# Outer sums of the weight: from adding DMAs to VectorE, in a list-scheduled factorization kernel

## Chip, cores and metric

One core of a Trainium2 chip. The metric is the device time of one execution in microseconds (us); the runs of the kernel before have a median of 1429.27 us (1428.62 to 1429.29, three runs).

## The reference

A factorization machine layer: a linear part, plus half the sum over 64 embeddings of the squared projection less the projection of squares. x is r_x, 1024 x 512; the weight is 64 x 512 x 512; all is float32.

```python
out_lin = x @ lin_w.T + lin_b
xv = jnp.einsum('bf,efm->bem', x, weight)
zp = jnp.einsum('bf,efm->bem', jnp.square(x), jnp.square(weight))
interaction = 0.5 * jnp.sum(jnp.square(xv) - zp, axis=1)
return out_lin + interaction
```

The second einsum needs only the sum of the weight's squares over the embeddings, so its product is small. The first is nearly all of the work.

## The kernel before

**Tiling.** The weight is rearranged on the host into 16 groups of 32 output columns, each a 512 x 2048 matrix (embedding within column). A group is cut into four quadrants w11, w12, w21, w22 (q = 0 to 3 of `weight[g, q]`), each 1 MB as 128 partitions x 2 column blocks x 2 x 512. For each group x times the matrix is made by two levels of a seven-product scheme (Strassen's, in Winograd's form). The outer level has seven products, in the order `ORDER` (line 19). The left operands X1 to X7 are sums of blocks of x, made once in the opening. The right operands are w11, w12, w21, w22 and outer sums: T1 of w11 and w12; T2 of T1 and w22; later w12 is overwritten by a sum with w22, and w21 by a sum with T2 (`outer_sum`, line 417). `RHS` (line 446) says which product i reads which.

**One outer product**, `tree` (line 450): GpSimd makes four inner sums t1 to t4 of the operand's blocks (128 x 512 each, two buffers each). Seven inner products follow, each one "pair" of the planner (`PAIR`, 1.72 in its units of us), which is four matmul instructions in the profile. `PLACE` (line 23) sets their order: product p of step s stands at 7s + PLACE[p], so that the inner products of neighbouring steps are interleaved. Their PSUM banks are b1, b3 and two of b2. Evacuations by ScalarE (`copy`) and VectorE bring the results to SBUF halves (128 x 1024): p5, p53, and the accumulators oa0 to oa3 and ob0 to ob3, one for each position pos of the four. `outer_psum` adds a bank to an accumulator; `outer_sbuf` adds a bank and p5 or p53, then (except where `early(pos)` holds) the accumulator, the latter with both inputs in SBUF. For outer products 2, 4, 5 and 3 `finish` squares the result on ScalarE and reduces it on VectorE into acc. `w_squares` squares and reduces the weight's quadrants likewise.

**early.** For pos 3 of products 2, 7, 4 and 3 the accumulator is added when p5 is evacuated (VectorE, one input in PSUM), so that the last addition with both inputs in SBUF falls away.

**Loads and outer sums before.** `load` brings a quadrant whole by SP's queue. T1 and T2 begin as a load of w11 from HBM into their own buffer, and `load_more` (line 409) then adds w12, or w12 and w22, to it by DMAs that accumulate, issued on GpSimd. w12 gets w22 added in the same way, w21 gets T2. With these sums (and not differences) the signs of X3, X5 and X6 are turned: `x_sum` makes "-a - b" on VectorE.

**The order of the work.** All work is entered in a `Plan` with its engines, a duration per engine, what it reads and writes. `Plan.order` (line 62) gives TensorE's order as fixed by the keys, works back the latest time of every other operation from it, and then steps through time: each engine that is free takes the ready operation with the earliest latest time. An operation that both VectorE and GpSimd can do is taken by VectorE only when it is urgent (line 122). The result is a fixed order for each engine. Lines 151 to 158 let an operation with two SBUF inputs (`both=True`) on VectorE and one on GpSimd lengthen each other:

```python
if e == DVE and o.both and free[POOL] > now + 0.1:
    over = free[POOL] - now
    cost += 0.9 * over
    longer(POOL, 0.35 * over)
elif e == POOL and free[DVE] > now + 0.1 and running[DVE].both:
```

`two_input` (line 272) gives the durations of additions: VectorE 0.08 + 1.06 and GpSimd 0.14 + 2.19 for 128 x 1024; with an input in PSUM, VectorE only. Every addition through it appears in the profile at line 280.

Of the kernel before, what the change touches and what calls it, by code (L numbers as in the profile page):

```python
# [12 lines left out]
AF = mybir.ActivationFunctionType  # L13
ALU = mybir.AluOpType
# [1 line left out]

P = 128
G = 2
ORDER = (1, 6, 2, 7, 5, 4, 3)

SLOT = {1: 0, 7: 1, 2: 2, 4: 3, 5: 4, 6: 5, 3: 6}

# [152 lines left out]
def kernel(  # L175
# [24 lines left out]

    nc = tc.nc  # L210
    NG, NQ, _, NCB, KH, N = weight.shape
    B = xT.shape[1]
# [21 lines left out]
    def make(name, shape, pool=sb):  # L234
        buf[name] = pool.tile(shape, F32, tag=name, name=name)
        return name
# [12 lines left out]
    for i in range(1, 8):  # L249
        make(f"X{i}", [P, 7, Q])  # L250
    for q in ("w11", "w12", "w21", "w22a", "w22b", "T1", "T2"):
        make(q, [P, 2, 2, N])
    for pos in range(4):
        make(f"oa{pos}", half)
        make(f"ob{pos}", half)
# [104 lines left out]

    for i, n in ((1, "A11"), (2, "A12"), (4, "A22")):
        act(block4(i), a_ap(n), None, a_parts(n), (f"X{i}",))

    def x_sum(i, o, a, b, kind, reads, size):

        if kind != "-a - b":
            costs, emit = two_input(o, a, b, kind == "a - b", size)
        else:
            costs = {DVE: two_input(o, a, b, True, size)[0][DVE]}

            def emit(_):
                nc.vector.scalar_tensor_tensor(o, a, -1.0, b, ALU.mult, ALU.subtract)

        plan.add(costs, emit, reads, (f"X{i}",), both=True)

    for i, a, b, kind in (
        (5, "A22", "A21", "a - b"),
        (6, "X5", "A11", "-a - b"),
        (7, "A11", "A21", "a - b"),
        (3, "X6", "A12", "-a - b"),  # L380
    ):
        x_sum(i, block4(i), a_ap(a), a_ap(b), kind, a_parts(a, b), 1024)
    for i in ORDER:
        x = buf[f"X{i}"]
        a11, a21, a12, a22 = (x[:, s, :] for s in range(4))
        s1, s2, s4 = (x[:, s, :] for s in range(4, 7))
        for o, a, b, kind in (
            (s1, a21, a22, "a + b"),
            (s2, s1, a11, "a - b"),
            (s4, a12, s2, "a - b"),  # L390
            (a21, a11, a21, "a - b"),
        ):
            x_sum(i, o, a, b, kind, (f"X{i}",), 256)
    for n in a_buf.values():
        plan.add({SP: 0.0}, None, (), (n,) + tuple((n, r) for r in range(KH)))
    for n in ("ob0", "ob1", "ob2", "ob3", "c_0", "c_1"):
# [5 lines left out]
    def w(g, q):  # L402
        return q + "ab"[g % 2] if q == "w22" else q

    def load(g, q):
        n = w(g, QUAD[q])
        dma(buf[n], weight[g, q], (), (n,), 4.8)

    def load_more(n, src, reads=()):

        plan.add(
            {POOL: 1.0},
            lambda _: nc.gpsimd.dma_start(buf[n], src, accum_op=ALU.add),  # L413
            (n,) + reads, (n,), land=8.0,
        )

    def outer_sum(g, which):
        if which < 3:
            n = f"T{which}"
            dma(buf[n], weight[g, 0], (), (n,), 4.8)  # L420
            for q in (1, 3)[:which]:
                load_more(n, weight[g, q])
        elif which == 3:
            load_more("w12", weight[g, 3])
        else:
            load_more("w21", buf["T2"], ("T2",))

    def w_squares(g, q):
        row, col = divmod(QUAD.index(q), 2)
        for c in range(NCB):  # L430
            n, sq = w(g, q), wsq_ring()
            act(buf[sq], buf[n][:, c], AF.Square, (n,), (sq,), 1.07)
            m = g * MG + (2 * col + c) * MI
            reduce(w2_sum[:, ts(row, KH), m:m + MI], buf[sq], (sq,), (("w2", row, m),))

# [6 lines left out]
        reduce(buf[acc_name[g]][:, b:b + G, m:m + MI], buf[n], (n,), ((acc_name[g], i, pos),))  # L442

    ADDEND = {6: "oa", 2: "oa", 7: "ob", 4: "oa", 3: "ob"}
    TARGET = {1: "oa", 6: "ob", 2: "oa", 7: "oa", 4: "oa", 3: "ob"}
    RHS = {1: "w11", 2: "w21", 3: "w22", 4: "w21", 5: "T1", 6: "T2", 7: "w12"}
    acc_name = {}
    acc_parts = [(i, pos) for i in (2, 3, 4, 5) for pos in range(4)]

    def tree(s, g, i):  # L450
        r = w(g, RHS[i])
        b11, b21, b12, b22 = (buf[r][:, c, k, :] for c in range(NCB) for k in range(KH))
        t = {k: t_ring[k]() for k in range(1, 5)}
        for k, a, b, reads in (
            (1, b12, b11, (r,)),
            (2, b22, buf[t[1]], (r, t[1])),
            (3, b22, b12, (r,)),
            (4, b21, buf[t[2]], (r, t[2])),
        ):
            costs, emit = two_input(buf[t[k]], a, b, True, 512)  # L460
            plan.add({POOL: costs[POOL]}, emit, reads, (t[k],))
        rhs = {
            1: (b11, r), 2: (b21, r), 3: (b22, r), 4: (buf[t[4]], t[4]),
            5: (buf[t[1]], t[1]), 6: (buf[t[2]], t[2]), 7: (buf[t[3]], t[3]),
        }

        def product(p, b, first):
            op, name = rhs[p]

            def emit(_):  # L470
                for j in range(G):
                    nc.tensor.matmul(  # L472
                        buf[b][:, j, :], buf[f"X{i}"][:, SLOT[p], ts(j, P)], op,
                        start=first, stop=True, skip_group_check=True,
                    )

            plan.add({PE: PAIR}, emit, (name, f"X{i}", b), (b,), key=7 * s + PLACE[p])

        def copy(o, b):
            act(buf[o], buf[b], None, (b,), (o,))  # L480

        def target(pos):
            return f"{TARGET[i]}{pos}"

        def early(pos):

            return pos == 3 and i in (2, 7, 4, 3)

        def outer_psum(b, pos):

            if i == 1:
                copy(f"oa{pos}", b)
            elif i == 5:
                o = c_ring()
                whole(o, f"oa{pos}", b, psum=True)
                whole(f"ob{pos}", f"ob{pos}", b, psum=True)
                finish(g, i, o, pos)
            else:
                o = target(pos)
                whole(o, b, f"{ADDEND[i]}{pos}", psum=True)  # L500
                if i in (2, 4, 3):
                    finish(g, i, o, pos)

        def outer_sbuf(b, p, pos):

            if i == 1:
                whole(f"oa{pos}", b, p, psum=True)
            elif i == 5:
                o = c_ring()
                whole(p, b, p, psum=True)  # L510
                whole(o, f"oa{pos}", p)
                whole(f"ob{pos}", f"ob{pos}", p)
                finish(g, i, o, pos)
            else:
                a, o = f"{ADDEND[i]}{pos}", target(pos)
                if early(pos):
                    whole(o, b, p, psum=True)
                else:
                    z = p if o == a else o
                    whole(z, b, p, psum=True)  # L520
                    whole(o, z, a)
                if i in (2, 4, 3):
                    finish(g, i, o, pos)

        b2, p5, p53 = b2_ring(), p5_ring(), p53_ring()
        product(5, "b3", True)
        if early(3):
            whole(p5, "b3", f"{ADDEND[i]}3", psum=True)
        else:
            copy(p5, "b3")  # L530
        product(3, "b3", False)
        copy(p53, "b3")
        product(1, "b1", True)
        copy(b2, "b1")
        product(6, b2, False)
        outer_sbuf(b2, p53, 1)
        product(2, "b1", False)
        outer_psum("b1", 0)
        product(7, b2, False)
        outer_sbuf(b2, p5, 3)  # L540
        product(4, b2, False)
        outer_psum(b2, 2)

    for g in range(NG):
        acc_name[g] = acc_ring()
        load(g, 0)
        outer_sum(g, 2)
        for q in (1, 2, 3):
            load(g, q)
        outer_sum(g, 1)  # L550
        w_squares(g, "w12")
        for idx, i in enumerate(ORDER):
            if i == 1:
                w_squares(g, "w11")
            if i == 2:
                w_squares(g, "w21")
            if i == 7:
                outer_sum(g, 3)
            if i == 4:
                outer_sum(g, 4)  # L560
            if i == 5:
                w_squares(g, "w22")
            tree(7 * g + idx, g, i)
        if g + 1 < NG:
            names = tuple((acc_name[g], *k) for k in acc_parts)
            dma(acc_dram[:, :, ts(g, MG)], buf[acc_name[g]], names, names + (("accd", g),))


    for n in ("w11", "w12", "w21", "T1", "T2", w(NG, "w22")):
        for c in range(2):  # L570
            buf[n, c] = buf[n][:, c]
        plan.add({SP: 0.0}, None, (), (n, (n, 0), (n, 1)))
    xe = {(h, q): (("w11", "w12")[h], q) for h in range(2) for q in range(2)}
    last = acc_name[NG - 1]
    edge = M - MG
    acc_all = tuple((n, c) for n in ("T2", w(NG, "w22")) for c in range(2))
    lin_all = tuple((n, c) for n in ("w21", "T1") for c in range(2))
    for (h, q), n in xe.items():
        dma(buf[n], x_src[:, ts(q, KH), ts(h, H)], (), (n,))
    for g in range(NB // G):  # L580
# [85 lines left out]
```

## Time and profile before

| | |
|---|---|
| median of three runs | 1429.27 us |
| profiled execution, its own time | 1429.27 us |
| its span, first to last instruction | 1427.5 us |
| granted TensorE clock, mean | 0.999 |
| TensorE busy | 1409.1 us (99%), 3264 matmuls |
| VectorE (DVE) busy | 1115.5 us (78%), 946 instructions |
| GpSimd (POOL) busy | 1010.6 us (71%), 703 instructions |
| ScalarE (ACT) busy | 678.8 us (48%), 692 instructions |
| DMA: accumulating and other transfers issued by GpSimd | 84.15 MB |
| DMA: transfers issued by SP and ACT | 115.09 MB |
| read from HBM | 177.34 MB |

The span is the time between the first and the last instruction on the chip; the execution's own time lies a little above it. In the profile's rows an engine is followed by the line, the operation, and "out<-in" by the tiles' names without their numbers (p stands for p5 and p53, b for the PSUM banks, t for the inner sums). A row's "idle before" is how long the engine stood before these instructions, and what it waited for.

### The profile page before, as it was taken

Reading aid. Unit: us, or ns where it says so; the run is one execution under the profiler, and the core shown is the slowest. Engines: PE = TensorE matmul, PEld = TensorE weight load, DVE = VectorE, ACT = ScalarE, POOL = GpSimd, SP = SyncE. Lnnn points to the kernel's source line nnn. Section 1 sums busy time; section 2 is a strip of 40 time slices with the busy share of each in tenths; the row PEclk is TensorE's granted clock in tenths of the full one; section 3 lists DMA queues with packets and bytes.
Section 4 is the critical chain, followed back from the end, with each engine's and each line's share of the span. In section 5 each row is a group of like instructions: output and inputs, shape, how many; then the busy total and the mean of one; then the engine's idle time right before and its main releaser. Section 6 shows DMA issues by size and latency. Waiting matters only on the chain.

```text
span 1427.5 us, 10368 instructions
## 1 busy us (share of the span) xinstructions
PE 1409.1 (99%) x3264; PEld 617.9 (43%) x3264; DVE 1115.5 (78%) x946; ACT 678.8 (48%) x692; POOL 1010.6 (71%) x703
## 2 busy tenths in 40 slices
PE   8999999999999999999999999999999999999998
PEld 3434444444444444444444444444444444444443
DVE  1779597886968779696877959788696978969785
ACT  1446354454635446364544635445463544636431
POOL 5886786857768686785958678685777868677660
PEclk9999999999999999999999999999999999999999
DMA  9656381745628175472836638274573817546331
GB/s 306 202 155 173 91 203 45 196 122 143 167 75 205 67 177 151 118 177 63 209 89 164 163 96 199 55 193 113 147 177 91 187 53 185 143 120 145 94 112 60
DMA packets 47286, 200.96 MB, mean 141 GB/s; under 512 B 19008, under 2 KB 20032, under 8 KB 24704
## 3 DMA queue, kind: packets, MB, share of 16 engines
q0 software_dynamic: 11600, 84.15, 30.2%
q1 hardware_dynamic: 35056, 115.09, 23.3%
q10 hardware_dynamic: 576, 1.05, 0.2%
q8 instruction: 27, 0.44, 0.1%
q14 instruction: 27, 0.22, 0.0%
HBM read 177.34 MB, written 6.16 MB: 129 GB/s over the span
## 4 chain that ended last, share of the span: by engine, by line
PE 92%; DMA 2%; POOL 2%; DVE 2%; issue 1%; ACT 0%; DVEq 0%; SPq 0%; ACTq 0%; POOLq 0%
PE b L472 90%; DMA T<-weight 2%; PE b L617 2%; DVE p L280 1%; POOL t L280 1%; POOL X L280 1%; DMA oa<-xT 0%; POOL ob L280 0%; DVE ob L280 0%; ACT X L293 0%; SPq L309 0%; POOL w L413 0%; DVE w22a L280 0%; DVEq L662 0%; ACTq L309 0%
## 5 line engine op out<-in xcount | busy, mean ns | idle before, releaser
L472 PE MATMUL b<-t,X 128*128 128x512 f32 x1792 | 806.1, 592 | 1.7 <-DVE ob L280 1.4
L472 PEld LDWEIGHTS b<-t,X 128*128 128x128 f32 x1792 | 339.2, 190 | 432.1 <-issue 419.9
L472 PE MATMUL b<-w,X 128*128 128x512 f32 x768 | 358.5, 592 | 3.4 <-DVE p L280 2.3
L280 POOL TENSOR_TENSOR t<-w 128x512 f32<-128x512 f32 x128 | 163.2, 1278 | 147.5 <-PE b L472 84.5
L472 PEld LDWEIGHTS b<-w,X 128*128 128x128 f32 x768 | 145.7, 190 | 187.8 <-issue 175.1
L293 ACT COPY p<-b 128x1024 f32<-128x1024 f32 x160 | 160.4, 1002 | 133.6 <-PE b L472 133.6
L295 ACT ACTIVATE oa<-oa 128x1024 f32<-128x1024 f32 x128 | 133.6, 1056 | 166.8 <-DVE oa L280 166.8
L280 POOL TENSOR_TENSOR t<-w,t 128x512 f32<-128x512 f32 x128 | 164.9, 1289 | 57.5 <-PE b L472 57.3
L472 PE MATMUL b<-T,X 128*128 128x512 f32 x384 | 180.4, 592 | 0.0
L302 DVE TENSOR_REDUCE acc<-oa 128x16 f32<-128x1024 f32 x128 | 152.1, 1208 | 18.0 <-ACT oa L295 18.0
L302 DVE TENSOR_REDUCE w_sum<-wsq 128x16 f32<-128x1024 f32 x128 | 152.8, 1204 | 0.2 <-ACT wsq L295 0.2
L293 ACT COPY b<-b 128x1024 f32<-128x1024 f32 x112 | 112.4, 1004 | 82.2 <-PE b L472 82.2
L280 DVE TENSOR_TENSOR oa<-b,p 128x1024 f32<-128x1024 f32 x96 | 116.6, 1214 | 34.7 <-PE b L472 34.7
L295 ACT ACTIVATE wsq<-w 128x1024 f32<-128x1024 f32 x96 | 98.0, 1054 | 70.0 <-DVE w_sum L302 66.5
L280 POOL TENSOR_TENSOR t<-T 128x512 f32<-128x512 f32 x64 | 83.5, 1305 | 47.5 <-issue 33.2
L295 ACT ACTIVATE c<-c 128x1024 f32<-128x1024 f32 x64 | 65.8, 1055 | 106.7 <-DVE c L280 102.8
L472 PEld LDWEIGHTS b<-T,X 128*128 128x128 f32 x384 | 73.0, 190 | 91.8 <-issue 88.2
L280 DVE TENSOR_TENSOR p<-b,p 128x1024 f32<-128x1024 f32 x80 | 97.3, 1216 | 17.9 <-PE b L472 17.9
L280 DVE TENSOR_TENSOR ob<-b,p 128x1024 f32<-128x1024 f32 x48 | 58.5, 1218 | 65.0 <-PE b L472 65.0
L295 ACT ACTIVATE ob<-ob 128x1024 f32<-128x1024 f32 x64 | 67.6, 1058 | 87.3 <-DVE ob L280 87.3
L280 DVE TENSOR_TENSOR oa<-b,oa 128x1024 f32<-128x1024 f32 x64 | 77.8, 1216 | 29.8 <-PE b L472 29.8
L280 POOL TENSOR_TENSOR t<-T,t 128x512 f32<-128x512 f32 x64 | 82.0, 1281 | 25.5 <-PE b L472 25.5
(55 smaller groups left out, 1328.4 us busy)
## 6 DMA issues: line engine op xcount, KB each, us to landing
w<-weight SPq DMA_DIRECT2D x48, 1024.0 KB, 4.9
T<-weight POOLq DMA_DIRECT2D x48, 1024.0 KB, 8.2
T<-weight SPq DMA_DIRECT2D x32, 1024.0 KB, 4.8
w<-weight POOLq DMA_DIRECT2D x16, 1024.0 KB, 10.8
w<-T POOLq DMA_DIRECT2D x16, 1024.0 KB, 6.9
w22a<-weight SPq DMA_DIRECT2D x8, 1024.0 KB, 6.1
w22b<-weight SPq DMA_DIRECT2D x8, 1024.0 KB, 5.9
w<-xT SPq DMA_DIRECT2D x4, 512.0 KB, 4.7
```

The costliest lines, as they stand in the source:

```text
L280: f(o, a, b)
L293: nc.scalar.copy(o, i)
L295: nc.scalar.activation(o, i, func)
L302: lambda _: nc.vector.tensor_reduce(o, i.rearrange("p a (m e) -> p a m e", e=E), axis=AX.X, op=ALU.add),
L472: nc.tensor.matmul(buf[b][:, j, :], buf[f"X{i}"][:, SLOT[p], ts(j, P)], op, start=first, stop=True, skip_group_check=True,)
L617: nc.tensor.matmul(buf[bank][:, j, :], buf[xe[h, k // KH]][:, k % KH, ts((g * G + j) % (NB // 2), P)], w2_sum[:, k, :], start=(k == 0), st ...
```

## The change

The diff, cut to its core. T1, T2 and the two later sums are made by VectorE from the loaded quadrants, as differences; each quadrant and each T becomes two tiles of half the size (suffix .0 and .1), with a load, a square and a sum each; `x_sum` with its turned signs goes, and the block sums of X may all be taken by either engine; `early` goes; product 4 comes before product 5; product 4 now ends in one of the c buffers and product 5 in oa, in place, where it was the other way round. `Plan`, `two_input`, `act` and `reduce` are the same in both.

```diff
-ORDER = (1, 6, 2, 7, 5, 4, 3)
+ORDER = (1, 6, 2, 7, 4, 5, 3)
...
     for q in ("w11", "w12", "w21", "w22a", "w22b", "T1", "T2"):
-        make(q, [P, 2, 2, N])
+        for c in range(NCB):
+            make(f"{q}.{c}", half)
...
-        (5, "A22", "A21", "a - b"),
-        (6, "X5", "A11", "-a - b"),
-        (7, "A11", "A21", "a - b"),
-        (3, "X6", "A12", "-a - b"),
...
+    for i, a, b, sub in ((5, "A21", "A22", 0), (6, "X5", "A11", 1), (7, "A11", "A21", 1), (3, "A12", "X6", 1)):
+        costs, emit = two_input(block4(i), a_ap(a), a_ap(b), sub)
+        plan.add(costs, emit, a_parts(a, b), (f"X{i}",), both=True)
...
-    def load(g, q):
-        n = w(g, QUAD[q])
-        dma(buf[n], weight[g, q], (), (n,), 4.8)
-
-    def load_more(n, src, reads=()):
-
-        plan.add(
-            {POOL: 1.0},
-            lambda _: nc.gpsimd.dma_start(buf[n], src, accum_op=ALU.add),
-            (n,) + reads, (n,), land=8.0,
-        )
+    def load(g):
+        for q in (0, 1, 3, 2):
+            for c in range(NCB):
+                n = f"{w(g, QUAD[q])}.{c}"
+                dma(buf[n], weight[g, q][:, c], (), (n,))
 
     def outer_sum(g, which):
-        if which < 3:
-            n = f"T{which}"
-            dma(buf[n], weight[g, 0], (), (n,), 4.8)
-            for q in (1, 3)[:which]:
-                load_more(n, weight[g, q])
-        elif which == 3:
-            load_more("w12", weight[g, 3])
-        else:
-            load_more("w21", buf["T2"], ("T2",))
+        o, a, b = {
+            1: ("T1", "w12", "w11"),
+            2: ("T2", w(g, "w22"), "T1"),
+            3: ("w12", w(g, "w22"), "w12"),
+            4: ("w21", "w21", "T2"),
+        }[which]
+        for c in range(NCB):
+            whole(f"{o}.{c}", f"{a}.{c}", f"{b}.{c}", True, DVE)
...
-    TARGET = {1: "oa", 6: "ob", 2: "oa", 7: "oa", 4: "oa", 3: "ob"}
+    TARGET = {1: "oa", 6: "ob", 2: "oa", 7: "oa", 3: "ob"}
...
         def target(pos):
-            return f"{TARGET[i]}{pos}"
-
-        def early(pos):
-
-            return pos == 3 and i in (2, 7, 4, 3)
+            return f"{TARGET[i]}{pos}" if i in TARGET else c_ring()
...
             elif i == 5:
-                o = c_ring()
-                whole(o, f"oa{pos}", b, psum=True)
-                whole(f"ob{pos}", f"ob{pos}", b, psum=True)
-                finish(g, i, o, pos)
+                for n in (f"oa{pos}", f"ob{pos}"):
+                    whole(n, n, b, psum=True)
+                finish(g, i, f"oa{pos}", pos)
...
                 a, o = f"{ADDEND[i]}{pos}", target(pos)
-                if early(pos):
-                    whole(o, b, p, psum=True)
-                else:
-                    z = p if o == a else o
-                    whole(z, b, p, psum=True)
-                    whole(o, z, a)
+                z = p if o == a else o
+                whole(z, b, p, psum=True)
+                whole(o, z, a)
...
-        if early(3):
-            whole(p5, "b3", f"{ADDEND[i]}3", psum=True)
-        else:
-            copy(p5, "b3")
+        copy(p5, "b3")
...
-        load(g, 0)
+        load(g)
+        outer_sum(g, 1)
         outer_sum(g, 2)
-        for q in (1, 2, 3):
-            load(g, q)
-        outer_sum(g, 1)
         w_squares(g, "w12")
```

More of the change, by code (lines that the diff above doesn't have):

```diff
@@ L362 @@
         act(block4(i), a_ap(n), None, a_parts(n), (f"X{i}",))
-    def x_sum(i, o, a, b, kind, reads, size):
-        if kind != "-a - b":
-            costs, emit = two_input(o, a, b, kind == "a - b", size)
-        else:
[L369 to L376, printed above, removed]
-        (5, "A22", "A21", "a - b"),
-        (6, "X5", "A11", "-a - b"),
-        (7, "A11", "A21", "a - b"),
-        (3, "X6", "A12", "-a - b"),
-    ):
-        x_sum(i, block4(i), a_ap(a), a_ap(b), kind, a_parts(a, b), 1024)
+    for i, a, b, sub in ((5, "A21", "A22", 0), (6, "X5", "A11", 1), (7, "A11", "A21", 1), (3, "A12", "X6", 1)):
+        costs, emit = two_input(block4(i), a_ap(a), a_ap(b), sub)
+        plan.add(costs, emit, a_parts(a, b), (f"X{i}",), both=True)
     for i in ORDER:
@@ L386 @@
         s1, s2, s4 = (x[:, s, :] for s in range(4, 7))
[L387 to L393, printed above, removed]
+        for o, a, b, sub in ((s1, a21, a22, 0), (s2, s1, a11, 1), (s4, a12, s2, 1), (a21, a11, a21, 1)):
+            costs, emit = two_input(o, a, b, sub, 256)
+            plan.add(costs, emit, (f"X{i}",), (f"X{i}",), both=True)
     for n in a_buf.values():
@@ L430, in w_squares @@
         for c in range(NCB):
-            n, sq = w(g, q), wsq_ring()
-            act(buf[sq], buf[n][:, c], AF.Square, (n,), (sq,), 1.07)
+            n, sq = f"{w(g, q)}.{c}", wsq_ring()
+            act(buf[sq], buf[n], AF.Square, (n,), (sq,), 1.07)
             m = g * MG + (2 * col + c) * MI
@@ L450, in tree @@
     def tree(s, g, i):
-        r = w(g, RHS[i])
-        b11, b21, b12, b22 = (buf[r][:, c, k, :] for c in range(NCB) for k in range(KH))
+        r = [f"{w(g, RHS[i])}.{c}" for c in range(NCB)]
+        b11, b21, b12, b22 = (buf[r[c]][:, k, :] for c in range(NCB) for k in range(KH))
         t = {k: t_ring[k]() for k in range(1, 5)}
         for k, a, b, reads in (
[L455 to L458, printed above, removed]
+            (1, b12, b11, (r[0], r[1])),
+            (2, b22, buf[t[1]], (r[1], t[1])),
+            (3, b22, b12, (r[1],)),
+            (4, b21, buf[t[2]], (r[0], t[2])),
         ):
@@ L462, in tree @@
         rhs = {
-            1: (b11, r), 2: (b21, r), 3: (b22, r), 4: (buf[t[4]], t[4]),
+            1: (b11, r[0]), 2: (b21, r[0]), 3: (b22, r[1]), 4: (buf[t[4]], t[4]),
             5: (buf[t[1]], t[1]), 6: (buf[t[2]], t[2]), 7: (buf[t[3]], t[3]),
@@ L508, in outer_sbuf @@
             elif i == 5:
-                o = c_ring()
                 whole(p, b, p, psum=True)
-                whole(o, f"oa{pos}", p)
-                whole(f"ob{pos}", f"ob{pos}", p)
-                finish(g, i, o, pos)
+                for n in (f"oa{pos}", f"ob{pos}"):
+                    whole(n, n, p)
+                finish(g, i, f"oa{pos}", pos)
             else:
                 a, o = f"{ADDEND[i]}{pos}", target(pos)
-                if early(pos):
-                    whole(o, b, p, psum=True)
-                else:
-                    z = p if o == a else o
-                    whole(z, b, p, psum=True)
-                    whole(o, z, a)
+                z = p if o == a else o
+                whole(z, b, p, psum=True)
+                whole(o, z, a)
                 if i in (2, 4, 3):
@@ L526, in tree @@
         product(5, "b3", True)
-        if early(3):
-            whole(p5, "b3", f"{ADDEND[i]}3", psum=True)
-        else:
-            copy(p5, "b3")
+        copy(p5, "b3")
         product(3, "b3", False)
@@ L566 @@
             dma(acc_dram[:, :, ts(g, MG)], buf[acc_name[g]], names, names + (("accd", g),))
[L569 to L573, printed above, removed]
+    xe = {(h, q): (f"w11.{q}", f"w12.{q}")[h] for h in range(2) for q in range(2)}
     last = acc_name[NG - 1]
     edge = M - MG
-    acc_all = tuple((n, c) for n in ("T2", w(NG, "w22")) for c in range(2))
-    lin_all = tuple((n, c) for n in ("w21", "T1") for c in range(2))
+    acc_all = ("T2.0", "T2.1", w(NG, "w22") + ".0", w(NG, "w22") + ".1")
+    lin_all = ("w21.0", "w21.1", "T1.0", "T1.1")
     for (h, q), n in xe.items():
```

## The prediction

> **What bounds the kernel now.** I read the granted clock first (0.999, so nothing is lost there), then the chain of waits that ended last, then one steady group of weights as a stretch, then VectorE and GpSimd in order of time inside it. The chain in order of time, from the steady part:
>
> ```profile
> 534.41 82.68 PE b L472 x192
> 617.10 0.03 issue
> 617.12 0.02 DVEq L280
> 617.14 0.58 issue
> 617.72 1.22 DVE p L280
> 618.94 0.04 issue
> 618.99 82.68 PE b L472 x192
> ```
>
> The reader should see that TensorE is the path: 192 matmuls in a row, one touch of VectorE, 192 again, repeating every 84.55 us. 82.68/192 is 0.4306 us a matmul; a group has 196, so 84.40 us is TensorE's own, and a group is held up by 0.15 us only. All 3264 matmuls at 0.4306 are 1405.5 us of the span of 1427.5; the other 22.0 are the head (6.0 before the first matmul), the opening and the tail. So the change can gain almost nothing in the steady part and can lose there if VectorE or GpSimd run out of idle time. How much they have, in that stretch:
>
> ```profile
> core 0: us, PE busy (x) PEld busy (x) DVE busy (x) ACT busy (x) POOL busy (x), PEclk, DMA share, GB/s
> 618.99:703.53 84.54, 84.38 (x196) 37.05 (x196) 68.08 (x58) 42.20 (x43) 61.47 (x44) 1.00 0.54 139
> ```
>
> VectorE is idle for 16.5 us of 84.5, GpSimd for 23.1, ScalarE for 42.3. Now the kind of operation the change adds. One VectorE addition with both inputs in SBUF is left in each group, and this is it, VectorE's rows and then GpSimd's:
>
> ```profile
> 696.53 1.21 DVE L302 TENSOR_REDUCE acc<-c 128x16 f32<-128x1024 f32 x1
> 697.65 3.56 DVE L280 TENSOR_TENSOR c<-oa,p 128x1024 f32<-128x1024 f32 x1
> 701.14 1.21 DVE L302 TENSOR_REDUCE w_sum<-wsq 128x16 f32<-128x1024 f32 x1
> 702.27 1.21 DVE L280 TENSOR_TENSOR p<-b,ob 128x1024 f32<-128x1024 f32 x1
> ```
>
> ```profile
> 697.52 2.61 POOL L280 TENSOR_TENSOR ob<-ob,p 128x1024 f32<-128x1024 f32 x1
> 700.08 2.27 POOL L280 TENSOR_TENSOR t<-w22b,t 128x512 f32<-128x512 f32 x1
> ```
>
> The same shape with one input in PSUM takes 1.21 us; this one takes 3.56, because it stands still until GpSimd's 2.61 us operation ends at 700.1, and then GpSimd's next (1.27 us elsewhere) takes 2.27. Each side waits for the other's instruction. The evacuation right behind it, p<-b,ob at 702.27, is the one that TensorE waits for at 703.5: one such addition per group, and one stall per group of 0.15 us.
>
> The Trainium skill says the same of the mechanism (SBUF — State Buffer, Who interferes with whom): a VectorE instruction with two SBUF inputs competes with a GpSimd instruction that reads SBUF, and the loser blocks wholly. By that rule alone the eight new sums would only queue with GpSimd: 61.5 - 4.3 + 9.4 + 8 x 1.2 = 76.2 us of 84.5, and nothing would be lost. The row of 3.56 us speaks against leaving it there, since VectorE stands idle while it queues, and the sum below goes by the rows.
>
> **The change part by part**, per group of 84.54 us.
>
> Rows of the groups that give prices:
>
> ```profile
> L280 DVE TENSOR_TENSOR c<-oa,p 128x1024 f32<-128x1024 f32 x15 | 53.7, 3581 | 0.0
> L280 DVE TENSOR_TENSOR p<-b,oa 128x1024 f32<-128x1024 f32 x32 | 38.9, 1216 | 36.3 <-PE b L472 36.3
> L280 POOL TENSOR_TENSOR oa<-p,oa 128x1024 f32<-128x1024 f32 x32 | 75.5, 2358 | 10.1 <-DVE p L280 8.2
> L280 POOL TENSOR_TENSOR t<-w 128x512 f32<-128x512 f32 x128 | 163.2, 1278 | 147.5 <-PE b L472 84.5
> L413 POOL DMA_DIRECT2D T<-weight x48 | 41.1, 856 | 5.2 <-DMA T<-weight 5.2
> ```
>
> 1. Adding DMAs removed: 48 + 16 + 16 issues on GpSimd over 16 groups, 5 each at 0.86: GpSimd -4.3 us. Two of six whole loads on SP's queue go and the four left become eight halves. The DMA engines are busy 0.54 of the stretch and no steady wait of TensorE names a DMA, so this gains nothing directly.
>
> 2. Eight sums (T1, T2, w12, w21, two halves each) on VectorE alone, both inputs in SBUF. Lower end: 1.21 each, the PSUM row, as if GpSimd were never in the way: 9.7. Upper end: 3.58 each, the row of c<-oa,p: 28.6. In between: GpSimd will have 28 operations of 1.27 and 14 of 2.36 per group, 68.6 us, so 0.81 of the time it is in one; what is left of it is (28 x 1.27² + 14 x 2.36²)/(2 x 68.6) = 0.90 on average, so a wait of 0.73 and 1.94 for a sum: 15.5. I take this, since the planner is free to place the sums and VectorE has gaps, where the one seen sits behind the longest kind.
>
> 3. The early merges undone (pos 3 of products 2, 7, 4, 3): four p<-b,oa or p<-b,ob leave VectorE, -4.9; four copies of 1.00 go to ScalarE, 46.2 of 84.5, hidden; four more additions of 2.36, most on GpSimd, +9.4.
>
> 4. GpSimd held by the eight sums: in the rows above 2.61 for 2.37 (the same addition just before it) and 2.27 for 1.27, so 1.24 each: +9.9 (lower end 0).
>
> Sums: VectorE 68.1 - 4.9 + 15.5 = 78.7 (72.9 to 91.8); GpSimd 61.5 - 4.3 + 9.4 + 9.9 = 76.5. Both at 90% or more, each in a fixed order, with TensorE needing banks back. How tight: by PLACE the bank b2 is read by VectorE between pairs 7s+3 and 7s+6, and 7s+6 and 7s+9, and b1 between 7s+4 and 7s+7, two pairs of 1.72 us free each, so 3.44 - 1.21 - some 0.3 of handing over leaves 1.9 us. A sum of 3.58 ahead of an evacuation overruns that, one of 1.94 ahead of a waiting one just about. Behind the late evacuation, the next product into that bank waits, and with it all of TensorE.
>
> 5. The order 4, 5 for 5, 4. w21 is read by product 2's last pair at 7s+4, then w21 - T2 is made, then GpSimd's first tree operation, then product 4, now two steps on, starts at 7s+8: three pairs, 5.2 us. Unhindered the chain is 0.4 (what GpSimd's rows behind TensorE stand idle) + 1.21 + 0.1 + 1.27 + 0.1 = 3.1; with the two rows of the collision 0.4 + 3.58 + 0.1 + 2.27 + 0.1 = 6.5. So 0 to 1.3 a group; I take 0.2, near the bottom, since the sum is short of time and the planner puts it first.
>
> 6. Stall per group, which no row shows for nine such additions. Lower end 0. Upper end VectorE's 91.8 - 84.4 = 7.4. I take 9 times the 0.17 that TensorE waits today behind one of them, 1.5, plus 0.2 from part 5: 1.7, near the lower row because the stretch still has 5.8 us of VectorE idle by the middle price. That is 1.55 more than now, over 16 groups 24.8 us.
>
> 7. Opening: TensorE now stands 1.10, 2.29 and 0.28 us, the last two after GpSimd waited 4.59 us for an adding DMA. That wait goes: up to -2.6. In its place four sums, and two block sums of X that may go to GpSimd at 2.63 us: up to +5.3, with GpSimd busy 34.0 of the 41 us from 36 to 77. I take 0. Tail: the last 1.41 us wait on VectorE stays, 0 (-1.4 to +2).
>
> Sum: span 1427.5 + 24.8 = 1452.3. The profiled execution took 1429.27 us by its own time, 1.77 above its span, and that is also the median of the runs: 1454.
>
> **The rivals.** (a) All hidden, and a little faster: the sums fall into the half of the group where VectorE now idles (16.5 us), GpSimd is rid of its issues and the opening of its DMA wait. At best the 2.4 us of steady stalls and 2.6 of the opening go: 1424; at worst nothing moves: 1432. For it: both engines stay below the group's length; against it: 3.56 for 1.21, and a stall behind it. It decides if the sums average no more than some 1.5 us and none stands before an evacuation. (b) VectorE becomes the bound: sums near 3.58 each, 91.8 per group: 16 x 7.4 = 118 more, 1547; half of it, 1488 to 1500, if the planner dodges some. For it: fifteen rows of fifteen took 3.56 to 3.60; against it: all fifteen are the same place in the order. (c) The words speak of a scheduler told of the contention, but lines 151 to 158 stand in both versions and the durations in two_input and reduce are not touched: then that part does nothing, and what acts is sums on VectorE, as costed.
>
> **How the numbers follow.** About 0.2% is what this kernel's measurement can tell from no change, 2.9 us. Forecast, a stall of 0.33 to 4.6 us a group: 0.71, 1432 to 1500. Rival (a): 0.17, of which 0.08 below 1426.4 and 0.09 inside 0.2%. Rival (b), above 1500: 0.12; (c) moves no time of its own. Slower is 0.83. The range 1430 to 1500 leaves out most of (a) and (b).
>
> **What would show it.** Right: one-input evacuations still 1.21, eight sums a group at 1.6 to 2.6 us, GpSimd's operations lengthened beside them, VectorE above 76 us a group, and the chain cut into several pieces per group by VectorE or GpSimd instead of one. Wrong: still 192 matmuls unbroken (rival a), or VectorE without idle time and groups of 90 us (rival b). If the loss sits in the first 77 us, part 7 was mis-sized; if TensorE waits for t after w21, part 5.

## The result and the profile after

The changed kernel takes 1438.50 us (median of 4 runs, 1438.25 to 1438.61) against 1429.13 for the kernel before on the same chip (4 runs): a ratio of 1.0066, 95% interval 1.0048 to 1.0083. It is slower, as forecast, but by 9.4 us where the prediction had 24.8. The profiled execution took 1438.61 us, its span 1436.8 against 1427.5 before.

The chain of waits of the changed kernel, in order of time (start, length, what), one group of the steady part. "issue" is time in which an engine waited for nothing that the profile shows, POOLq is the queue of GpSimd; where the chain goes from one engine to another in mid-operation, it shows only the end of that operation:

```profile
634.18 79.25 PE b L438 x184
713.43 0.03 POOLq L274
713.46 0.60 POOL t L274
714.06 3.30 POOL oa L274
717.36 0.02 issue
717.38 0.02 ACT oa L289
717.40 0.94 issue
718.34 1.00 ACT p L287
719.34 0.04 issue
719.39 79.25 PE b L438 x184
```

There is still one break per group, and a group is 85.21 us where it was 84.55. But it is another break than before: no longer a VectorE evacuation, but GpSimd's addition to oa, then a square on ScalarE, then ScalarE's copy to p5. TensorE's own wait there is 0.82 us (0.17 before). The same stretch as a whole:

```profile
core 0: us, PE busy (x) PEld busy (x) DVE busy (x) ACT busy (x) POOL busy (x), PEclk, DMA share, GB/s
634.14:719.35 85.21, 84.38 (x196) 37.15 (x196) 76.27 (x62) 46.50 (x47) 69.36 (x42) 1.00 0.17 51
```

TensorE's 84.38 us are unchanged; VectorE has 8.9 us left and GpSimd 15.9. So neither is full. What goes wrong is in the order of time at the end of the group, VectorE first, then GpSimd, ScalarE and TensorE:

```profile
706.08 1.21 DVE L274 TENSOR_TENSOR w12.1_75<-w22a.1_79,w12.1_75 128x1024 f32<-128x1024 f32 x1
...
711.16 1.77 DVE L274 TENSOR_TENSOR T1.0_82<-w12.0_74,w11.0_72 128x1024 f32<-128x1024 f32 x1
712.86 2.28 DVE L274 TENSOR_TENSOR ob<-ob,p 128x1024 f32<-128x1024 f32 x1
715.06 3.36 DVE L274 TENSOR_TENSOR T2.0_84<-w22a.0_78,T1.0_82 128x1024 f32<-128x1024 f32 x1
```

```profile
706.31 3.21 POOL L274 TENSOR_TENSOR oa<-oa,p 128x1024 f32<-128x1024 f32 x1
709.48 2.38 POOL L274 TENSOR_TENSOR ob<-ob,p 128x1024 f32<-128x1024 f32 x1
711.80 2.25 POOL L274 TENSOR_TENSOR t<-w11.1_73 128x512 f32<-128x512 f32 x1
714.02 3.33 POOL L274 TENSOR_TENSOR oa<-oa,p 128x1024 f32<-128x1024 f32 x1
```

```profile
711.74 1.00 ACT L287 COPY b<-b 128x1024 f32<-128x1024 f32 x1 [0.18 <-PE b L438]
717.38 1.06 ACT L289 ACTIVATE oa<-oa 128x1024 f32<-128x1024 f32 x1 [4.64 <-POOL oa L274]
718.34 0.99 ACT L287 COPY p<-b 128x1024 f32<-128x1024 f32 x1
```

```profile
719.39 1.98 PE L438 MATMUL b<-w11.1_73,X 128*128 128x512 f32 x4 [0.82 <-ACT p L287]
```

Read it from the bottom. TensorE needs bank b3 back from the copy to p5 for the next group's first product. The copy stands behind the square of oa on ScalarE, which has waited 4.64 us for GpSimd's addition to oa. GpSimd is done with that addition late because three of its last four operations took 3.21, 2.25 and 3.33 us for 2.37, 1.27 and 2.37: at each, a VectorE addition with two SBUF inputs was running or next in turn (w12.1, T1.0, and the addition to ob). In these rows VectorE and GpSimd take strict turns. T1.0, from 711.16, stands until ob<-ob,p ends at 711.86, then runs; GpSimd's t, from 711.80, stands until T1.0 ends at 712.93; VectorE's ob stands until t ends at 714.05; and so on. Each turn costs GpSimd 0.84 to 0.98 us.

The difference of the spans, 9.3 us, from TensorE's rows in both profiles: 15 times (0.82 - 0.17) in the steady part, +9.75; the first matmul at 7.90 us instead of 5.96, +1.94; the opening's stalls of 2.29 and 0.28 gone, -2.57; the linear part 30.23 instead of 30.43, -0.2; two single waits of 0.4 and 0.2 that are new, both near the end, +0.6. Together 9.5.

### The profile page after: what moved, and what is told of

Read it like the earlier page. It is cut to its first block, busy times and chain, and to the rows that moved or that the text cites. A ratio compares the mean times of both kernels' runs of the same rounds, so it can differ in the third digit from the quotient of the medians.

```text
span 1436.8 us, 10763 instructions
## 1 busy us (share of the span) xinstructions
PE 1408.8 (98%) x3264; PEld 619.3 (43%) x3264; DVE 1245.7 (87%) x1006; ACT 748.8 (52%) x756; POOL 1149.6 (80%) x691
## 4 chain that ended last, share of the span: by engine, by line
PE 90%; POOL 4%; DVE 2%; issue 1%; ACT 1%; DMA 1%; DVEq 0%; POOLq 0%; SPq 0%
PE b L438 86%; POOL oa L274 3%; PE b L325 2%; PE b L565 2%; ACT p L287 1%; POOL t L274 1%; DMA ob<-lin_wT 0%; DVE p L274 0%; DMA T1.1_83<-lind 0%; DVE ob L274 0%; DVE w11.1_73 L536 0%; DVE w21.0_76 L274 0%; DVE oa L274 0%; DVE acc L296 0%; DVE w11.0_72 L536 0%
## 5 line engine op out<-in xcount | busy, mean ns | idle before, releaser
L287 ACT COPY p<-b 128x1024 f32<-128x1024 f32 x224 | 225.6, 1007 | 266.1 <-PE b L438 226.8
L438 PE MATMUL b<-w21.0_76,X 128*128 128x512 f32 x256 | 120.3, 592 | 0.0
L274 POOL TENSOR_TENSOR oa<-oa,p 128x1024 f32<-128x1024 f32 x32 | 102.8, 3212 | 1.8
L274 POOL TENSOR_TENSOR oa<-p,oa 128x1024 f32<-128x1024 f32 x32 | 75.7, 2365 | 27.2 <-DVE p L274 26.9
L274 POOL TENSOR_TENSOR c<-c,oa 128x1024 f32<-128x1024 f32 x32 | 75.4, 2357 | 13.8 <-DVE c L274 11.7
L274 POOL TENSOR_TENSOR oa<-oa,ob 128x1024 f32<-128x1024 f32 x32 | 76.4, 2387 | 6.9 <-DVE oa L274 6.9
L274 POOL TENSOR_TENSOR ob<-ob,oa 128x1024 f32<-128x1024 f32 x32 | 76.3, 2384 | 5.5 <-DVE ob L274 5.5
L274 POOL TENSOR_TENSOR ob<-p,ob 128x1024 f32<-128x1024 f32 x32 | 75.7, 2364 | 0.5 <-DVE p L274 0.5
L296 DVE TENSOR_REDUCE acc<-ob 128x16 f32<-128x1024 f32 x64 | 75.9, 1209 | 0.0
L296 DVE TENSOR_REDUCE acc<-c 128x16 f32<-128x1024 f32 x64 | 74.8, 1208 | 1.1 <-ACT c L289 1.1
```

Source lines behind the costliest of these rows:

```text
L274: f(o, a, b)
L287: nc.scalar.copy(o, i)
L296: lambda _: nc.vector.tensor_reduce(o, i.rearrange("p a (m e) -> p a m e", e=E), axis=AX.X, op=ALU.add),
L438: nc.tensor.matmul(buf[b][:, j, :], buf[f"X{i}"][:, SLOT[p], ts(j, P)], op, start=first, stop=True, skip_group_check=True,)
```

## The experiments

Each is the changed kernel with one edit, unless it says otherwise; the time of the kernel before beside them was 1428.9 to 1429.8 us.

**The copy first.** The order is the planned one; only two neighbours on ScalarE change places.

```diff
+        if tag[a] == ("sq", 5) and tag[b] == ("p5", 1):
...
+            seq[a:b + 1] = seq[a + 1:b + 1] + [seq[a]]
```

> Edit: on ScalarE the copy that evacuates b3 to p5 for product 1 goes ahead of the square of product 5's oa that now stands before it; nothing else moves. Theory Q (the loss is a wait in ScalarE's fixed order: the square waits 4.6 us for GpSimd's held addition, the copy behind it is late, TensorE stands 0.82 us a group): the 15 stalls of 0.82 go, 1438.5 - 12.3 = 1426 (1425 to 1428), the chain runs through 196 matmuls a group with 0.2 us or less of stall. Rival C (VectorE and GpSimd are short of room as such, and this copy only happens to be what is late first): the stall comes back a few pairs later, 1434 to 1439.

Measured: 1424.41 us, ratio to the kernel before 0.9964 (0.9951 to 0.9977). The chain runs without a break through nearly all groups:

```profile
46.36 1281.38 PE b L439 x2980
```

So rival C falls: nothing else comes late. In that chain a group of 196 matmuls takes 1281.38/2980 x 196 = 84.28 us; against it the break costs 85.21 - 84.28 = 0.93 a group, 14.0 us over 15 groups, which is what the exchange gained (1438.50 - 1424.41 = 14.1). But theory Q was not wholly right either. ScalarE's rows of this run:

```profile
710.85 1.01 ACT L287 COPY p<-b 128x1024 f32<-128x1024 f32 x1 [4.64 <-POOL oa L274]
711.76 1.06 ACT L289 ACTIVATE oa<-oa 128x1024 f32<-128x1024 f32 x1
```

The copy, put first, waits the same 4.64 us for the same addition. p5 has two buffers, and product 5's, two steps back, is the one the copy writes: GpSimd's addition still reads it. The exchange gained one ScalarE instruction, about a microsecond, and that was enough.

**Which of the two holds the copy.** p5 in three buffers (the third holds the bias in the opening), the planner still planning with two: once in the order of the changed kernel, once with the copy first.

```diff
+    p5_real = ring("p5r", 3, half)
...
+        buf[p5] = buf[p5_real()]
```

> Edit: the changed kernel in its own order, but with p5 in three buffers in turn instead of two (the third holds the bias in the opening); the planner still plans with two. In e1_copy_first the copy that was put first still waited 4.6 us for GpSimd's oa addition, which reads the p5 buffer that the copy is to write. Theory F (both waits hold: the square waits for the addition's output, the copy for its input buffer; the square in front costs one ScalarE instruction on top): with the buffer free the square still stands in front, 1437 to 1439, 0.8 us a group. Rival G (the buffer alone is the wait): 1421 to 1426.

> Edit: three p5 buffers and the copy put ahead of the square. Theory F: only with both is the copy free: it starts some 4 us earlier against TensorE's need than in e1_copy_first, without a wait for GpSimd; the time is TensorE's floor as there, 1421 to 1425. Rival: the copy still waits for GpSimd, by something else.

Measured: 1438.55 (0.8 us a group at the copy, as before the edit) and 1422.22 us. In the second, ScalarE's copy is free of GpSimd:

```profile
705.70 1.01 ACT L294 COPY p5r<-b 128x1024 f32<-128x1024 f32 x1 [0.72 <-PE b L446]
709.63 1.06 ACT L296 ACTIVATE oa<-oa 128x1024 f32<-128x1024 f32 x1 [2.92 <-POOL oa L281]
```

TensorE needs the bank at 710.65 in that run, so the copy has 4 us to spare. Theory F holds: two waits for one GpSimd addition, one for its output (the square) and one for its input (the buffer). Taking away either alone leaves the other.

**Which sums cost.** Half sums on VectorE are replaced by a copy of the same size with one SBUF input (the difference is left out, T or w holds one operand); the order stays. The edit, here with the condition of the first of these runs; the others differ in the condition alone:

```diff
             whole(f"{o}.{c}", f"{a}.{c}", f"{b}.{c}", True, DVE)
+            if which < 3:
+                x, y = buf[f"{o}.{c}"], buf[f"{a}.{c}"]
+                plan.ops[-1].emit = lambda _, x=x, y=y: nc.vector.tensor_reduce(
+                    x.rearrange("p a (m e) -> p a m e", e=1),
+                    y.rearrange("p a (m e) -> p a m e", e=1), axis=AX.X, op=ALU.add
+                )
```

> Edit: the four half sums T1 and T2 of each group become VectorE reductions over one element, a copy of the same size with one input in SBUF, so T1 and T2 hold w12 and w22 alone; the order is that of the changed kernel. Theory Q: these four are the ones that stand beside GpSimd's additions of product 5; they take 1.2 us each, GpSimd's oa addition 2.4 for 3.3, the stall of 0.82 goes: 1426 to 1428. Rival P (each SBUF sum costs its share, as the prediction took it, 9.3 us over eight sums): half the loss, 1433 to 1435.

> Edit: as the run before, but for the other four half sums, w12 - and w21 -, which become copies of one input; T1 and T2 stay sums. Theory Q: they stand elsewhere in the group, nothing is gained, 1438.5 within 1, stall still 0.8 a group at the copy to p5. Rival P: half the loss, 1433 to 1435.

Measured: 1424.30 and 1421.97 us. The second was a miss: w12's half 1 does stand beside those operations of GpSimd, at 706.08 ahead of the first. Either four take away all of the stall (TensorE's rows name no steady wait in either run), 14.2 and 16.5 us, so that the two gains together are about twice what is lost. A share per sum can't do that; a threshold can, and theory S was made from it:

> Edit: six of the eight half sums become copies of one input (both of T2 and of w21, T1's half 1, w12's half 0); only T1's half 0 and w12's half 1 stay sums. Theory S (the loss is a threshold: GpSimd's run of four operations up to product 5's last oa addition is held about a microsecond each by w12's half 1, T1's half 0 and the addition to ob on VectorE, the square and the copy behind it come 0.82 us too late, and sums that stand elsewhere cost nothing): 1437 to 1439, TensorE still stands 0.8 us a group at the copy to p5. Rival P (shares): six eighths of the loss go, 1426 to 1429.

> Edit: one of the eight half sums, w12's half 1, becomes a copy of one input; the other seven stay sums. Theory S: GpSimd's run comes 0.85 us earlier, more than the 0.82 that TensorE waits, so all of the loss goes with this one: 1421 to 1426. Rival P: an eighth goes, 1436 to 1438.

> Edit: one of the eight half sums, T1's half 0, becomes a copy of one input; the other seven stay sums. Theory S: as with w12's half 1, all of the loss goes: 1421 to 1426. Rival P: 1436 to 1438.

Measured: 1437.42 with six of eight replaced, 1423.06 with w12's half 1 alone, 1423.95 with T1's half 0 alone. TensorE's waits with six replaced (engine, line, released by: total, times, longest), the same 16 as in the changed kernel:

```profile
PE b L444 <- ACT p L287: 13.5, 16, 1.1
```

and GpSimd and ScalarE with w12's half 1 alone replaced:

```profile
699.24 2.37 POOL L274 TENSOR_TENSOR oa<-oa,p 128x1024 f32<-128x1024 f32 x1
...
705.11 3.34 POOL L274 TENSOR_TENSOR oa<-oa,p 128x1024 f32<-128x1024 f32 x1
```

```profile
708.48 1.06 ACT L289 ACTIVATE oa<-oa 128x1024 f32<-128x1024 f32 x1 [2.82 <-POOL oa L274]
```

The first addition takes 2.37 again for 3.21. GpSimd's run is 0.84 us shorter from there on, and that covers the 0.82. With T1's half 0 replaced the first addition still takes 3.21, and it is t that is short again:

```profile
705.16 1.26 POOL L274 TENSOR_TENSOR t<-w11.1_73 128x512 f32<-128x512 f32 x1
```

It takes 1.26 us for 2.25 with TensorE's products around it unchanged, so its length was VectorE's doing and not a wait for TensorE, from which the chain above enters it. Six sums cost 1.1 us between them, which the intervals of the two runs do not tell from nothing, and each of two single ones decides over 15: 15.4 and 14.6.

The runs of the changed kernel without a steady stall lie between 1422.0 and 1424.6 us. A group of unbroken matmuls takes 84.14 us in the run with the planner's delay below, 84.18 with w12's half 1 replaced, 84.28 with the exchange, 84.31 with the old order restored. Most of this difference is stalls too short for a row to name. TensorE's starts with the exchange, and then with the planner's delay:

```profile
710.16 1.88 PE L439 MATMUL b<-w22b.0_80,X 128*128 128x512 f32 x4
711.91 1.99 PE L439 MATMUL b<-w11.1_73,X 128*128 128x512 f32 x4
713.74 1.88 PE L439 MATMUL b<-t,X 128*128 128x512 f32 x4
```

```profile
709.66 1.88 PE L436 MATMUL b<-w22b.0_80,X 128*128 128x512 f32 x4
711.38 1.88 PE L436 MATMUL b<-w11.1_73,X 128*128 128x512 f32 x4
713.10 1.88 PE L436 MATMUL b<-t,X 128*128 128x512 f32 x4
```

Undisturbed products start 1.72 us apart. With the exchange the product that reuses the bank starts 1.75 us after the one before it, and the next 1.83 us later: 0.14 us lost, which is 84.28 - 84.14. The copy there ends at 711.86, just before the start at 711.91. So even a copy in time to 0.05 us costs a little, and a break costs more than the wait that its row names: 85.21 - 84.14 = 1.07 us a group in the changed kernel, and 84.55 - 84.14 = 0.41 in the kernel before.

**The planner's delay.** Only the four numbers in lines 151 to 158 (146 to 153 in the changed kernel) are set to what the rows show.

```diff
-                        cost += 0.9 * over
-                        longer(POOL, 0.35 * over)
+                        cost += over
...
-                        cost += 0.5 * over
-                        longer(DVE, 0.9 * over)
+                        cost += over
```

> Edit: in the planner alone, the mutual delay is set to what the rows of the changed kernel show, whoever starts second waits out the first (cost plus all of the remaining time) and the first is not lengthened, for 0.9/0.35 and 0.5/0.9. Theory Q: the order was planned with GpSimd about a microsecond early at this place; planned with the measured exclusion the square is not put ahead, and the time is 1425 to 1431. Rival C: there is no order without a stall, 1435 to 1442.

> Edit: the kernel before with the planner's mutual delay as measured (the edit of e4_lock). Theory S: the 0.17 us a group behind the one addition on VectorE go, 15 x 0.17 = 2.5, and the opening's two stalls of 2.6 us, which hang on the adding DMAs, stay: 1426 to 1428, still above e4_lock. Rival O (the opening's stalls are the planner's too): 1423 to 1425, level with e4_lock.

Measured: 1422.83 us for the changed kernel (ratio to before 0.9952, 0.9938 to 0.9967), but 1442.86 for the kernel before (1.0093, 1.0076 to 1.0109). In the first, ScalarE's rows are not as theory Q had them:

```profile
708.86 1.06 ACT L287 ACTIVATE oa<-oa 128x1024 f32<-128x1024 f32 x1 [3.15 <-POOL oa L272]
710.00 1.01 ACT L285 COPY p<-b 128x1024 f32<-128x1024 f32 x1
```

The square still stands ahead of the copy. What moved is GpSimd's t, which now comes behind the addition to oa; the addition ends at 708.83, and the copy is done at 711.01, 0.37 us before TensorE starts on the bank.

The second was a miss for both theories. Its steady part has one wait of 1.30 us a group, and VectorE's rows say why:

```profile
702.32 3.57 DVE L278 TENSOR_TENSOR c<-oa,p 128x1024 f32<-128x1024 f32 x1
705.81 1.21 DVE L300 TENSOR_REDUCE w_sum<-wsq 128x16 f32<-128x1024 f32 x1
706.94 1.20 DVE L278 TENSOR_TENSOR c<-oa,b 128x1024 f32<-128x1024 f32 x1
708.07 1.21 DVE L278 TENSOR_TENSOR p<-b,ob 128x1024 f32<-128x1024 f32 x1
```

The addition still takes 3.57 us (GpSimd's ob<-ob,p began 0.13 us ahead of it), and the new order puts another addition, c<-oa,b, ahead of the evacuation that TensorE waits for. The opening, on the other hand, lost its two stalls with the adding DMAs all kept: TensorE's rows from its first product of group 1 to that group's end name only the 1.10 us that every version has, though GpSimd still waits 4.7 us for one of these DMAs.

> Edit: e10_before_lock, with the evacuation to p5 of product 3 put ahead of product 5's c addition that stands before it on VectorE in the new order; nothing else. Theory: the 13.7 us that the measured exclusion cost the kernel before are this one place, where TensorE stands 1.30 us a group: it falls by one VectorE instruction, 1.13, to 0.17, 1442.9 - 15 x 1.13 = 1426 (1425 to 1430). Rival: other places in the new order are late too, 1434 to 1441.

Measured: 1436.49 us, where the rival had it and 10 us above the theory. The place is right, the 1.30 falls to 0.20 in the group shown, but the moved addition now makes the next evacuation late:

```profile
619.88 1.98 PE L470 MATMUL b<-w22a,X 128*128 128x512 f32 x4 [0.20 <-DVE p L278]
622.24 1.95 PE L470 MATMUL b<-t,X 128*128 128x512 f32 x4 [0.37 <-DVE p L278]
```

The third place for c<-oa,b, behind both evacuations, is that of the kernel before, in its own order:

```profile
703.40 1.21 DVE L280 TENSOR_TENSOR p<-b,p 128x1024 f32<-128x1024 f32 x1
704.53 1.20 DVE L280 TENSOR_TENSOR c<-oa,b 128x1024 f32<-128x1024 f32 x1
```

```profile
703.53 1.98 PE L472 MATMUL b<-w22b,X 128*128 128x512 f32 x4 [0.17 <-DVE p L280]
```

There TensorE waits only the 0.17 us. So the more exact numbers led the planner to a worse place for this one instruction.

**The other parts of the change.** First the order 5, 4, the c buffers and the early merges restored in the changed kernel, so that the sums, the halved tiles and the signs are left; then the same with the planner's delay as measured; then the kernel before with the early merges undone.

```diff
-ORDER = (1, 6, 2, 7, 4, 5, 3)
+ORDER = (1, 6, 2, 7, 5, 4, 3)
...
+                if early(pos):
+                    whole(o, b, p, psum=True)
```

```diff
-            return pos == 3 and i in (2, 7, 4, 3)
+            return False
```

> Edit: the changed kernel with product 5 before 4 again, ending in a c buffer, and with the early merges, so that of the change only the sums on VectorE, the halved tiles and the signs are left. Theory S: the steady floor is TensorE's, any stall hangs on what the planner puts beside one run; with 9.4 us less on GpSimd a group the run has room: 1421 to 1427. Rival W (the prediction's part 5: with w21 ready three pairs before product 4 no longer, but with early evacuations on VectorE, the sums now stand ahead of four more evacuations): 1432 to 1440.

> Edit: e8_order_early with the planner's mutual delay as measured. Theory S: e8_order_early already stands at TensorE's floor in the steady part, nothing is left for the planner: 1422 to 1425. Rival C: the two together leave room for another order that is better by more than 2 us: below 1422.

> Edit: the kernel before with the early merges undone alone (the prediction's part 3 by itself: 64 evacuations go from VectorE to ScalarE's copies, 64 additions of 2.36 us come, most to GpSimd); the sums stay with the adding DMAs. Theory S: product 4's or 3's additions lengthen GpSimd's run by 2.4 us a step where an evacuation needs them, so it may show a stall or none by where the planner puts them; GpSimd has 61.5 + 9.4 = 70.9 of 84.5 us, so none by capacity: 1427 to 1432. Rival: with the DMA issues on the same queue the run is too long, 1435 to 1445.

Measured: 1424.59, 1424.07 and 1426.63 us (ratio of the last 0.9976, 0.9966 to 0.9987). With the order and the merges of before, the sums on VectorE cause no steady stall that a row names. What is left is 84.31 - 84.14, 0.17 us a group, and it is of the kind that the prediction looked for: T1's half 0 takes 2.61 us on VectorE, the evacuation behind it ends at 694.42, and TensorE's row there takes 5.49 us for 5.31. The kernel before gets rid of its 0.17 us a group when the merges go, with GpSimd at 70.8 us a group. Single waits of up to 2.8 us stay in its opening, and up to 1.4 at its end. Its nine runs lie between 1423.44 and 1428.57, wider apart than those of any other version here; the runs do not show why.

**The first load.**

> Edit: e4_lock, with ScalarE's second load of x issued after its first copy instead of at 1.2 us. The first matmul starts at 7.9 us after the change and at 6.0 before it. Theory H (the four loads in flight at once make the first lin_wT land later): it starts at 6 to 7 us and the time is 1420 to 1421.5. Rival: it is SP's third load, of x instead of the weight, that is in the way, and the start stays at 7.9 to 8.6, 1422 to 1424.

The second of ScalarE's load instructions goes behind its first copy in the emitted order. Measured: 1420.70 us, ratio to before 0.9940 (0.9925 to 0.9955), the best of all. The first matmul, in the run with the planner's delay alone and in this one:

```profile
8.64 30.23 PE L323 MATMUL b<-ob,oa 128*128 128x512 f32 x64 [8.64 <-DMA ob<-lin_wT]
```

```profile
6.53 29.60 PE L324 MATMUL b<-ob,oa 128*128 128x512 f32 x64 [6.53 <-DMA ob<-lin_wT]
```

Theory H holds: the load of lin_wT, issued at 1.2 us in both, lands 2.1 us earlier with one transfer less beside it. In the twelve traces of the changed kernel and its versions with the load at its old place, the first matmul starts at 7.8 to 8.6 us. In the kernel before, where ScalarE issues that load only at 7.5 us, it starts at 6.0.

## Why the prediction was right and wrong

**What bounds the kernel: right, with the floor a little too high.** The 84.40 us were taken from a chain that has one restart in it; where nothing is late, a group takes 84.14. So the kernel before loses 0.41 us a group, not 0.15, and the unbroken versions reach 1422.0, below the 1424 that rival (a) had at best.

**Parts 1 to 4, the prices: right for VectorE, too high for GpSimd.** Four of the twelve rows of the eight sums (a sum that reads w22 has two, one for w22a and one for w22b):

```profile
L274 DVE TENSOR_TENSOR w21.0_76<-w21.0_76,T2.0_84 128x1024 f32<-128x1024 f32 x16 | 33.3, 2080 | 0.0
L274 DVE TENSOR_TENSOR T1.0_82<-w12.0_74,w11.0_72 128x1024 f32<-128x1024 f32 x16 | 28.2, 1763 | 17.7 <-DMA w12.0_74<-weight 17.7
L274 DVE TENSOR_TENSOR T2.0_84<-w22b.0_80,T1.0_82 128x1024 f32<-128x1024 f32 x8 | 26.9, 3364 | 0.0
L274 DVE TENSOR_TENSOR w12.1_75<-w22a.1_79,w12.1_75 128x1024 f32<-128x1024 f32 x8 | 9.7, 1213 | 0.0
```

Over all twelve the mean is 1.84 us (1.94 predicted), from 1.21 to 3.36. VectorE has 76.3 us a group (78.7 predicted), GpSimd 69.4 (76.5). Part 4 let all eight sums hold GpSimd, 1.24 us each, 9.9; in the group shown four of its operations are held, 0.84 to 0.98 us each, 3.8 together. The Trainium skill (SBUF — State Buffer, Who interferes with whom) has it that the instruction that starts first keeps the shared reads and the other blocks; both cases are in the rows above, w12.1 at 1.21 us with GpSimd held, T1.0 at 1.77 with GpSimd first.

**Part 5: wrong, and small.** GpSimd waits for w21's half 0, up to 1.2 us, but TensorE nowhere waits behind it; 0.2 was expected.

**Part 6 failed: "I take 9 times the 0.17 that TensorE waits today behind one of them, 1.5, plus 0.2 from part 5: 1.7".** Measured: 0.82, which is 0.65 more than before where 1.55 was forecast. The size is off by half, but the kind is off too. The stall does not grow here with the number of additions: six of eight sums replaced took 1.1 us off the time, one of eight took 15.4 off. Nor is the late operation of the changed kernel an evacuation behind a sum on VectorE, as argued from PLACE; it is ScalarE's copy, behind a square and a buffer that both hang on GpSimd. The prediction looked for the delay on the engine that gets the new work. It arose on the engine that is held by it, and reached TensorE over a third.

**Part 7: 0 taken, and 0 came out, by luck.** The opening gained 0.6, the sum of a later first load (+1.9), which has no term in the prediction, and the stalls that went (-2.6); the two new waits near the end took the 0.6 back. The adding DMAs alone were not the cause of the stalls, as the kernel before with the other planner's delay shows: same DMAs, no such stalls.

**The rivals.** The forecast's side was right and its size was not, and the side was in part luck: rival (a), all hidden and 1424, is what the changed kernel does as soon as one of several small things is altered, two neighbours on ScalarE, one sum, four numbers of the planner. It was priced to within some 2 us and given 0.17; that the loss hung on a single place in the order was not seen. Rival (b) fell: VectorE keeps 8.9 us a group. Rival (c), that the planner's part is no part of this change, holds as far as the code goes, but the planner's four numbers turned out to be worth 15.7 us in the changed kernel.

## What to carry to other kernels

When the bounding engine is already at its floor and others are merely busy, do not price added work by a stall apiece: find the one chain that ends at a deadline, and ask how much room it has and which operations beside it can hold it. Follow the delay to the engine that is held, not only to the one that got the work, and look there for two waits on the same event, such as an output and a reused buffer. Compare the starts of the bounding engine's operations too, since a wait too short to be named can still cost time in every group. A fixed order that is planned needs the durations and delays that the profile shows, but each plan must be timed: the more exact numbers gained 15.7 us in one version and lost 13.7 in the other.

## What was not expected of the hardware

That one of the two engines would be held was expected; how evenly and at what price was not. At additions with SBUF inputs VectorE and GpSimd take turns instruction by instruction, and the one that runs is not slowed: 1.21 us on VectorE stays 1.21 when it starts first (w12.1, 0.23 us ahead of GpSimd's addition), and becomes 3.56 when the row of GpSimd's addition starts 0.13 us before it. A few tenths of a microsecond in the start thus decide over 2.4 us, and over which of the two engines pays.
